# Attention over a graph: degree rows shared between two engines, and strip 0 checked early

## The chip, the cores and the metric

One Trainium2 chip, one core of it. The time is that of the device in microseconds (us) from launch to end; the profile's span runs from the first to the last instruction of one profiled execution. A core has TensorE (PE; its weight loads are listed as PEld), VectorE (DVE), ScalarE (ACT), GpSimd (POOL) and SyncE (SP, here used only to issue transfers). Each engine works through its own queue in order; semaphores tie the queues together.

## The reference

A graph of 2708 nodes with 128 features each: `x` (2708 x 128) and a dense 0/1 matrix `adj` (2708 x 2708, float32). Layer 0, which the change touches:

```
deg = clip(adj.sum(axis=1), 1);  dis = deg ** -0.5
diffusion = (dis[:, None] * adj * dis[None, :]) @ x - x
sim  = x @ x.T / (|x_i| |x_j|)
attn = softmax(beta * sim * adj, axis=1)
x = layernorm(x + diffusion + sigmoid(alpha) * (attn @ x - x))
```

Layer 1 is a second attention with `den = exp(leaky_relu(s_row + s_col))`, `att = den / (A @ den)`, `H = A @ (att @ (x W))`, and a last layernorm. It takes the larger part of the time and isn't changed.

## The kernel before

Nodes are cut into 22 blocks of 128 rows (the last has 20), and the columns of the transposed adjacency matrix into strips of 512 columns: strips 0 to 4, and a side strip 5 of 148 columns.

**Attention.** One loop runs over the strips in the order 2, 3, 4, 1, 0; I call its passes places 0 to 4. Place 4, the last, works on strip 0. In each place 22 steps `k` run over the blocks in the order 8 to 21, 4 to 7, 0 to 3 (`taken`). A step computes a 128 x 512 tile of similarities `sim` on PE (or turns one that an earlier place has kept), multiplies it on DVE with `gentle` (the limited beta) and with the block's piece of the adjacency matrix (`p_t`, line 651), takes the exponential in place on ACT (`grown`, 681), adds it on POOL to `total`, which becomes the softmax denominator, and multiplies it on PE with x into `att_acc` (`weighed`, 692). `p_t` has six buffers, `sim` four PSUM banks. Place 3 is wide: it carries the side strip along, and its `total` lies in `x1`, which has no other use yet.

The pieces of the current strip lie in `kept_a`, six tiles by groups of four blocks (2, 3, 4, 5, 1, 0 in the order of use); SP reloads each as soon as its last block is used. In place 4 there is no next strip to load.

**Degree rows.** `degree` (503) loads half a row block of `adj` (128 x 1354) into one of three rooms in turn and sums it on ACT into `deg2`. There are 44 of these; `rows_at` says at which steps of which place each is asked for. `roots` turns ready degrees into `dis` (DVE, then a power on POOL), at step 11 of place 2, step 20 of place 3 and step 12 of place 4. In place 4, at steps 11, 15, 19 and 21, x is scaled by `dis` on DVE (742), for blocks that att_acc no longer needs unscaled.

**What place 4 prepares.** `round_part(g)` copies a group of strip 0 into the matmul's rounded format on DVE; `check_part(g)` sums the low bits of the same pieces on ACT, so that a matrix that isn't exact in the short format is noticed; only then can `load_part(1, g)` let POOL's DMA queue load strip 1 into the group's place. `rounded_at` and `checked_at` hold the steps. Groups 2 and 3 of strip 1 are asked for at steps 17 and 20. Groups 1 and 0 are checked, and the other four loads are asked for, only after the place, behind the side strip's diffusion (1014 to 1021).

**Diffusion.** From line 1009 on PE multiplies each strip with x in two halves (`x_hi`, `x_lo`, made on DVE at 795 from the scaled x): side strip, 0, 1, 2, then 3 and 4. Strip s + 2 is loaded into the room of strip s as its parts are used up. `attended` finishes a strip of the attention: it sums `total` over the partitions on PE, turns `att_acc`, and adds the result to `att`. For strip 0 that is called after the side strip's diffusion and ahead of strip 0's in the text of the program.

**Order.** The order of each engine's queue is fixed when the program is built, by a planner that goes by the order of the text, its own costs and the times at which it thinks inputs are there. `in_order` pins a function's instructions behind the newest `p_t` product, exponential or addition of the place on their engine; they may be put later than that, not earlier. So the step numbers are the earliest places, not the real ones.

```
        def in_order(f):
            latest.update(behind)
            strict.append("some")
            f()
            strict.pop()
```

Of the kernel before, what the change touches and what calls it, by code (L numbers as in the profile page):

```python
# [12 lines left out]
I16 = mybir.dt.int16  # L13
AF = mybir.ActivationFunctionType
ALU = mybir.AluOpType
# [3 lines left out]
P = 128  # L19
N = 2708  # L20
D = 128
NB = (N + P - 1) // P
NP = NB * P
LAST = N - (NB - 1) * P
SW = 512
# [22 lines left out]
def grouped(  # L48
# [15 lines left out]
    nc = tc.nc  # L64
# [129 lines left out]
    def pinned(engine, op, *args, **kwargs):  # L194
        with ExitStack() as e:
            if engine in latest:
                e.enter_context(tc.issue_after(latest[engine].ins))
            latest[engine] = op(*args, **kwargs)  # L198
            return latest[engine]
# [9 lines left out]
    def dve(op, *args, **kwargs):  # L209
        if strict:  # L210
            return pinned("DVE", getattr(nc.vector, op), *args, **kwargs)
        return getattr(nc.vector, op)(*args, **kwargs)  # L212

    def act(op, *args, **kwargs):
        if strict:
            return pinned("ACT", getattr(nc.scalar, op), *args, **kwargs)
        return getattr(nc.scalar, op)(*args, **kwargs)  # L217

    def gps(op, *args, **kwargs):
        if strict:  # L220
            return pinned("POOL", getattr(nc.gpsimd, op), *args, **kwargs)
        return getattr(nc.gpsimd, op)(*args, **kwargs)  # L222
# [12 lines left out]
    def to_sbuf(acc, v, nb):  # L235

        t = lp.tile([P, SW], F32, tag="to_rows", name="tr_sb", bufs=2)
        if v < nb * P:
            nc.gpsimd.memset(t[:, v : nb * P], 0.0)
        act("copy", t[:, :v], acc[:, :v])  # L240
        return t
# [8 lines left out]
    def turned(t, nb):  # L250

        rows = tp_bank("tr_ps")
        for b in range(nb):
            mm(nc.tensor.transpose, rows[:, b, :], t[:, ts(b, P)], ident)
        return rows
# [78 lines left out]
    with ExitStack() as es:  # L334
# [161 lines left out]
# [4 lines that stand above are left out]
            f()  # L500
            strict.pop()

        def degree(ib, h):

            if (2 * ib + h) % 3 < 2:
                z = row_rooms[(2 * ib + h) % 3]
            else:
                z = x1[:, 6:, :].rearrange("p b i -> p (b i)")[:, : N // 2]
            nc.sync.dma_start(z, adj[ts(ib, P), h * (N // 2) : (h + 1) * (N // 2)])
            pinned(  # L510
                "ACT", nc.scalar.activation, z, z, AF.Copy,
                accum_out=deg2[:, ib, h : h + 1],
            )

        def roots(b0, b1):

            t = deg[:, b0:b1]
            dve("tensor_tensor", t, deg2[:, b0:b1, 0], deg2[:, b0:b1, 1], ALU.add)
            dve("tensor_scalar", live[:, b0:b1], t, 0.0, None, ALU.is_gt)
            dve("tensor_scalar", t, t, 1.0, None, ALU.max)  # L520
            gps("tensor_tensor", dis[:, b0:b1], t, minus_half[:, b0:b1], ALU.pow)

        def attended(s, acc, total):

            v, nb = width(s), blocks(s)
            sums = tp_bank("sums")
            for b in range(nb):
                nc.tensor.matmul(
                    sums[:, b, 0:1], total[:, ts(b, P)], ones[:, 0:1], start=True, stop=True
                )  # L530
            rsum = small.tile([P, SW // P], F32, tag="rsum", name="rsum")
            nc.vector.reciprocal(rsum[:, :nb], sums[:, :nb, 0])
            nc.vector.tensor_scalar(rsum[:, :nb], rsum[:, :nb], sig, None, ALU.mult)
            rows = turned(to_sbuf(acc, v, nb), nb)
            for b in range(nb):
                ib = s * 4 + b
                r = att[:, ib, :]
                nc.vector.scalar_tensor_tensor(
                    r, rows[:, b, :], rsum[:, b : b + 1], r, ALU.mult, ALU.add
                )  # L540


        room_of = {2: "room5", 3: "room1", 4: "room3", 1: "room0", 0: "room4", 5: "room2"}
        rounded_at = {2: 5, 3: 8, 4: 12, 1: 15, 0: 18, 5: 19}
        checked_at = {2: 13, 3: 18, 4: 21, 5: 21}
        strips = {0: {}, NS - 1: kept_c}

        def part_of(s, g):
# [7 lines left out]
        def round_part(g):  # L556
            dve("tensor_copy", part_of(0, g), kept_a[g])

        def check_part(g, room=None):
            low_bits_of(  # L560
                kept_a[g].rearrange("p b i -> p (b i)"),
                room or row_rooms[g % 2].bitcast(I16),
            )

        def load_part(s, g):
            src = adj_t[4 * g * P : min(4 * g + 4, NB) * P, ts(s, SW)]
            pinned(
                "strips", gps, "dma_start", part_of(s, g),
                src.rearrange("(b p) i -> p b i", p=P),
            )  # L570
# [6 lines left out]
        ended = []  # L577
        scaled = set()
        for n, s in enumerate(order):
# [2 lines left out]
            acc = ps_acc.tile([P, SW], F32, tag="acc", name="att_acc")  # L582
            if wide:
                total = x1[:, :6, :].rearrange("p b i -> p (b i)")
                nc.gpsimd.memset(total[:, w_all:], 1.0)
                tp_tags.remove("tp2")
                acc_side = ps_tp.tile([P, SW], F32, tag="tp2", name="att_acc_side")
            else:
                total = lp.tile([P, SW], F32, tag="total", name="total", bufs=2)
            gps("memset", total[:, :w_all], 0.0)  # L590

            prep = {
                (0, 1): lambda: normalize(12, 16),
# [6 lines left out]
                (1, 17): lambda: constants(2),  # L600
                (2, 11): lambda: roots(0, 8),
                (3, 20): lambda: roots(8, 18),
                (4, 12): lambda: roots(18, NB),
            }

            rows_at = {
                0: (18, 20), 1: range(0, NB, 2), 2: range(0, NB, 2),
                3: [k for k in range(21) if k % 3 < 2], 4: range(0, 12, 2),
            }
            turns = {  # L610
                3: lambda: turn_rows(12, 16, by_dve),
# [20 lines left out]
            for k, jb in enumerate(taken):  # L632
# [87 lines left out]
                if wide and k == 7:  # L720
                    in_order(lambda: attention_starts(NS - 1))
                if k in rows_at[n]:
                    in_order(lambda: degree(*todo.pop(0)))
                if n == len(order) - 1:
                    for g in [g for g, at in rounded_at.items() if at == k]:
                        in_order(lambda: round_part(g))
                    if k in (17, 20):
                        in_order(lambda: load_part(1, groups[k > 17]))
                    for g in [g for g, at in checked_at.items() if at == k]:
                        in_order(lambda: check_part(g))  # L730
                    if k in (11, 15, 19, 21):

                        done = sorted(taken[: k + 1 if k == NB - 1 else k - 1])
                        done = [b for b in done if b not in scaled]
                        scaled.update(done)
                        while done:
                            b0 = b1 = done[0]
                            while b1 in done:
                                done.remove(b1)
                                b1 += 1  # L740
                            xs = x_sb[:, b0:b1, :]
                            nc.vector.tensor_tensor(
                                xs, xs,
                                dis[:, b0:b1].unsqueeze(2).to_broadcast([P, b1 - b0, D]),
                                ALU.mult,
                            )
# [262 lines left out]
    for s in (NS - 1, 0, 1, 2):  # L1009
        acc = ps_acc.tile([P, SW], F32, tag="acc", name="dif_acc")  # L1010
        diffuse(s, acc)
        if s < 3:
            load_strip(s + 2)
        if s == NS - 1:
            attended(*ended.pop())
            for g in (1, 0):
                check_part(
                    g, work2.tile([P, 2048], I16, tag="low", name="low_junk", bufs=1)
                )
            for g in groups[2:]:  # L1020
                load_part(1, g)
        if s == 1:
            flat = kept_c.rearrange("p b i -> p (b i)")
            v = SHORT
            for b0, b1 in ((0, NB // 2), (NB // 2, NB)):
                low_bits_of(
                    flat[:, b0 * v : b1 * v],
                    work2.tile([P, 2048], I16, tag="low", name="low_junk", bufs=1),
                )
        normed(s, summed_up(s, acc))  # L1030
        x1_t = x1_in_sbuf(s, x1_turned(s))
        pbs = []
        for k in (1, 0):
            pb = scores(s, x1_t, k, score_bank())
            tally(s, pb, k)
            pbs.append(pb)
        shared_row(s, pbs[0])
        picked(s, pbs[0], sr_p)
        picked(s, pbs[1], sc_p)
        limited(s * 4, s * 4 + blocks(s))  # L1040
        e2(s * 4, s * 4 + blocks(s))
        if s == 1:
            fill("e")
# [1146 lines left out]
```

## Time and profile before

| what | us |
|---|---|
| median of 3 runs | 654.78 (653.06 to 657.62) |
| the profiled execution | 655.02 |
| its span | 653.6 |
| PE busy in the span | 611.0 (93%) |
| DVE busy | 492.1 (75%) |
| ACT busy | 471.1 (72%) |
| POOL busy | 291.2 (45%) |
| first p_t product of place 4 (DVE) | 175.0 |
| last p_t product of place 4 (DVE) | 207.7 |
| last att_acc product begins (PE) | 214.2 |
| first product of strip 0's diffusion (PE) | 221.1 |
| last degree row on ACT ends | 202.4 |

Lines of a timeline give the start, the duration, engine, source line, operation and its tiles; in brackets stands how long the engine was idle before and what released it. Many lines bear L198, L207 or L222, since these are the helpers that record every operation: tiles tell them apart. A busy share is an average over stages with different limits, and matmul ends are modelled, so PE can be shown busy where it partly waits.

### The profile page before, as it was taken

The page shows a single profiled execution, that of the slowest core. Times are in us where ns is not written, and L with a number is a line of the kernel's source. Part 1 is how long each engine was busy: PE and PEld are TensorE (multiplying, and loading weights), DVE is VectorE, ACT ScalarE, POOL GpSimd, SP SyncE. Part 2 cuts the span into 40 slices and gives each one's busy share as a digit, 9 for nine tenths or more (in the row PEclk, how much of TensorE's full clock was granted, in tenths as well). Part 3 has the DMA queues.
Part 4 walks back from the last instruction along what each step waited for, and adds up shares of the span by engine and source line. Part 5 has one row for each costly group of instructions (what it writes and reads, how often), then busy time and mean ns, then how long its engine had stood idle before and what let it go on. Part 6 is the DMA issues. An engine that isn't in the chain of part 4 may idle for free.

```text
span 653.6 us, 8554 instructions
## 1 busy us (share of the span) xinstructions
PE 611.0 (93%) x2859; PEld 354.7 (54%) x2859; DVE 492.1 (75%) x978; ACT 471.1 (72%) x649; POOL 291.2 (45%) x270
## 2 busy tenths in 40 slices
PE   8999999999999899988768899999999999989993
PEld 5445444475655676756645344444444444658872
DVE  4765875764699756757585999999999999498574
ACT  3857786777889521411376999999999999778662
POOL 5977778777798742000113323333232230022573
PEclk9999999999999899999879999999999999999997
DMA  8968989998972999988869997666689553359971
GB/s 273 385 209 319 323 291 366 357 342 299 335 260 76 274 389 390 386 274 301 330 247 251 252 231 234 183 180 177 195 216 266 173 165 128 98 206 384 390 296 53
DMA packets 66407, 171.64 MB, mean 263 GB/s; under 512 B 10059, under 2 KB 19285, under 8 KB 63333
## 3 DMA queue, kind: packets, MB, share of 16 engines
q1 hardware_dynamic: 42500, 107.01, 46.5%
q0 software_dynamic: 22464, 62.25, 33.9%
q10 hardware_dynamic: 1392, 1.77, 0.9%
q8 instruction: 24, 0.39, 0.2%
q14 instruction: 27, 0.21, 0.1%
HBM read 171.89 MB, written 5.72 MB: 272 GB/s over the span
## 4 chain that ended last, share of the span: by engine, by line
PE 75%; DVE 8%; POOL 6%; ACT 5%; issue 3%; DMA 2%; DVEq 0%; POOLq 0%; SPq 0%; ACTq 0%
PE num L198 15%; PE m_acc L198 15%; PE att_acc L207 9%; PE h_acc L1685 7%; PE sim L207 7%; PE dif_acc L207 6%; POOL total L222 4%; PE tot L198 2%; DMA nat<-in_adj_t 2%; PE sim L198 2%; DVE q L198 1%; PE dif_acc L198 1%; PE idle_ps L198 1%; ACT xn L198 1%; PE att_acc L198 1%
## 5 line engine op out<-in xcount | busy, mean ns | idle before, releaser
L198 PE MATMUL m_acc<-q,xws 128*128 128x512 f32 x240 | 121.6, 592 | 0.0
L222 POOL TENSOR_TENSOR total<-total,p_t 128x512 f32<-128x512 f32 (+1 forms) x67 | 91.7, 1369 | 21.0 <-ACT p_t L217 18.3
L198 PE MATMUL num<-ring,wt 128*128 128x512 f32 x216 | 98.1, 546 | 3.0 <-DVE q L198 2.2
L207 PE MATMUL att_acc<-p_t,x_sb 128*128 128x512 f32 x184 | 91.1, 602 | 1.1 <-ACT p_t L217 1.1
L212 DVE SCALAR_TENSOR_TENSOR p_t<-sim,gentle,pieces 128x512 f32<-128x512 f32 x89 | 65.0, 745 | 34.9 <-PE sim L207 25.7
L198 DVE SCALAR_TENSOR_TENSOR q<-sr_b,nc_s,q 128x1536 f32<-128x1536 f32 (+1 forms) x48 | 77.8, 1623 | 16.5 <-ACT q L198 16.5
L217 ACT ACTIVATE p_t<-p_t,shift 128x512 f32<-128x512 f32 (+1 forms) x89 | 64.7, 745 | 33.3 <-DVE p_t L212 31.0
L198 DVE COPY q<-num 128x512 f32<-128x512 f32 (+1 forms) x142 | 83.4, 611 | 3.7 <-PE num L198 3.7
L198 PEld LDWEIGHTS m_acc<-q,xws 128*128 128x128 f32 x240 | 45.3, 190 | 55.0 <-issue 55.0
L198 ACT ACTIVATE q<-q,head,rest 128x1536 f32<-128x1536 f32 (+1 forms) x48 | 70.2, 1508 | 1.5 <-DVE ring L198 1.2
L198 ACT ACT_TABLE_LOAD x52 | 66.7, 1283 | 3.9 <-issue 3.1
L198 PEld LDWEIGHTS num<-ring,wt 128*128 128x128 f32 x216 | 39.0, 190 | 48.4 <-issue 34.2
L198 ACT ACTIVATE q<-q,c_s 128x1536 f32<-128x1536 f32 (+1 forms) x48 | 62.9, 1355 | 0.3
L198 POOL DMA_INDIRECT ring<-in_adj_t,k_no x18 | 21.9, 1217 | 85.8 <-PE num L198 84.9
L207 PEld LDWEIGHTS att_acc<-p_t,x_sb 128*128 128x128 f32 x184 | 31.6, 190 | 35.4 <-ACT p_t L217 19.1
L207 PE MATMUL sim<-xn_t 128*128 128x512 f32 x98 | 47.6, 592 | 0.0
L222 POOL TENSOR_TENSOR x<-x,p_t 128x660 f32<-128x660 f32 (+1 forms) x22 | 35.1, 1595 | 11.3 <-ACT p_t L217 10.6
L198 ACT ACTIVATE row<-row 128x1354 f32<-128x1354 f32 x30 | 39.5, 1319 | 0.6 <-DMA row<-in_adj 0.6
L207 PE MATMUL dif_acc<-strip,x_hi 128*128 128x512 f32 x88 | 37.7, 429 | 0.0
L207 PE MATMUL dif_acc<-strip,x_lo 128*128 128x512 f32 x88 | 36.4, 414 | 0.0
L1685 PE MATMUL h_acc<-rounded,m_hi 128*128 128x512 f32 x88 | 32.5, 407 | 3.7 <-DVE rounded L212 3.7
L198 POOL DMA_INDIRECT xws<-xw_d,j_no x24 | 27.5, 1147 | 16.3 <-DVE c_s L198 9.3
(362 smaller groups left out, 1185.7 us busy)
## 6 DMA issues: line engine op xcount, KB each, us to landing
pieces<-in_adj_t SPq DMA_DIRECT2D x24, 1024.0 KB, 6.4
strip<-in_adj_t POOLq DMA_DIRECT2D x20, 1024.0 KB, 18.3
row<-in_adj SPq DMA_DIRECT2D x30, 677.0 KB, 6.0
nat<-in_adj_t SPq DMA_DIRECT2D x18, 768.0 KB, 6.1
x<-in_adj SPq DMA_DIRECT2D x14, 677.0 KB, 5.8
ring<-in_adj_t SPq DMA_DIRECT2D x9, 1024.0 KB, 5.1
x_sb<-in_adj_t SPq DMA_DIRECT2D x5, 768.0 KB, 6.3
pieces<-in_adj_t SPq DMA_DIRECT2D x7, 512.0 KB, 5.8
```

Of the source, the lines that this page charges most:

```text
L198: latest[engine] = op(*args, **kwargs)
L207: op(*args, **kwargs)
L212: return getattr(nc.vector, op)(*args, **kwargs)
L217: return getattr(nc.scalar, op)(*args, **kwargs)
L222: return getattr(nc.gpsimd, op)(*args, **kwargs)
L1685: nc.tensor.matmul(acc[:, : rows.shape[-1]], m[:, kb, :], rows, start=(kb, part) == (0, 0), stop=(kb, part) == (NB - 1, 1),)
```

## The change

Five edits, all in the attention's loop and right behind it:

- `degree` takes a flag; where it is set, the half row is summed by a DVE scalar operation with an accumulated sum instead of by ACT. `rows_by_dve` names the steps. The rows' steps change too: more in places 1 and 2, three instead of six in place 4.
- The last `roots` goes from step 12 to step 7 of place 4.
- `rounded_at` and `checked_at` get earlier steps, and all six groups are checked within the place, in the row rooms. A new table `asked_at` asks for each group of strip 1 some steps behind its check.
- The two memsets of the wide `total` are pinned at the start of place 3.
- `attended` of strip 0 is called after strip 0's diffusion; only its copy of `att_acc` to SBUF stays behind the side strip's.

```
-        def degree(ib, h):
+        def degree(ib, h, by_dve):
...
-            pinned(
-                "ACT", nc.scalar.activation, z, z, AF.Copy,
-                accum_out=deg2[:, ib, h : h + 1],
-            )
+            into = deg2[:, ib, h : h + 1]
+            if by_dve:
+                dve("tensor_scalar", z, z, 1.0, 0.0, ALU.mult, ALU.add, accum_out=into)
+            else:
+                act("activation", z, z, AF.Copy, accum_out=into)
...
-        def attended(s, acc, total):
+        def attended(s, acc, total, t=None):
...
-            rows = turned(to_sbuf(acc, v, nb), nb)
+            rows = turned(t or to_sbuf(acc, v, nb), nb)
...
-        rounded_at = {2: 5, 3: 8, 4: 12, 1: 15, 0: 18, 5: 19}
-        checked_at = {2: 13, 3: 18, 4: 21, 5: 21}
+        rounded_at = {2: 3, 3: 5, 4: 8, 1: 11, 0: 14, 5: 18}
+        checked_at = {2: 4, 3: 6, 4: 9, 1: 12, 0: 15, 5: 19}
+        asked_at = {2: 9, 3: 10, 4: 13, 1: 16, 0: 19, 5: 21}
...
-                nc.gpsimd.memset(total[:, w_all:], 1.0)
+                in_order(lambda: gps("memset", total[:, w_all:], 1.0))
...
-            gps("memset", total[:, :w_all], 0.0)
+            if wide:
+                in_order(lambda: gps("memset", total[:, :w_all], 0.0))
+            else:
+                gps("memset", total[:, :w_all], 0.0)
...
-                (4, 12): lambda: roots(18, NB),
+                (4, 7): lambda: roots(18, NB),
...
-                0: (18, 20), 1: range(0, NB, 2), 2: range(0, NB, 2),
-                3: [k for k in range(21) if k % 3 < 2], 4: range(0, 12, 2),
+                0: (18, 20), 1: (*range(0, NB, 2), 21), 2: (*range(0, NB, 2), 5, 13),
+                3: [k for k in range(21) if k % 3 < 2], 4: (0, 2, 4),
+            }
+            rows_by_dve = {
+                0: (), 1: (4, 8, 12, 16, 20), 2: (2, 5, 8, 11, 13, 14, 20),
+                3: (1, 4, 7, 10, 13, 16, 19), 4: (0, 2, 4),
...
-                    in_order(lambda: degree(*todo.pop(0)))
+                    in_order(lambda: degree(*todo.pop(0), k in rows_by_dve[n]))
...
-                    if k in (17, 20):
-                        in_order(lambda: load_part(1, groups[k > 17]))
                     for g in [g for g, at in checked_at.items() if at == k]:
                         in_order(lambda: check_part(g))
+                    for g in [g for g, at in asked_at.items() if at == k]:
+                        in_order(lambda: load_part(1, g))
...
         if s == NS - 1:
-            attended(*ended.pop())
-            for g in (1, 0):
-                check_part(
-                    g, work2.tile([P, 2048], I16, tag="low", name="low_junk", bufs=1)
-                )
-            for g in groups[2:]:
-                load_part(1, g)
+            in_sbuf = to_sbuf(ended[0][1], SW, SW // P)
+        if s == 0:
+            attended(*ended.pop(), in_sbuf)
```

More of the change, by code (lines that the diff above doesn't have):

```diff
@@ L557, in round_part, with check_part @@
             dve("tensor_copy", part_of(0, g), kept_a[g])
-        def check_part(g, room=None):
+        def check_part(g):
             low_bits_of(
                 kept_a[g].rearrange("p b i -> p (b i)"),
-                room or row_rooms[g % 2].bitcast(I16),
+                row_rooms[g % 2].bitcast(I16),
             )
```

## The prediction

> **What bounds the kernel now.** I read the page first, then the windows by stage, the chain of waits, and the timelines of DVE and PE around the end of the last place. The windows by place of the attention (places 1 to 3, place 4, the gap to the diffusion, the diffusion) give, in us, PE, PEld, DVE, ACT and POOL busy with their counts, the granted clock, the DMA share and GB/s:
>
> ```profile
> 50.00:92.00 42.00, 41.99 (x120) 19.16 (x119) 30.41 (x60) 30.82 (x48) 30.50 (x26) 1.00 0.87 316
> 92.00:129.00 37.00, 36.69 (x120) 18.23 (x119) 23.46 (x41) 26.85 (x42) 29.92 (x24) 1.00 1.00 360
> 129.00:174.00 45.00, 44.70 (x203) 28.46 (x201) 27.41 (x56) 33.91 (x47) 33.93 (x22) 1.00 0.90 322
> 174.00:209.00 35.00, 34.38 (x153) 20.65 (x152) 31.28 (x47) 31.82 (x50) 30.71 (x21) 1.00 0.63 209
> 209.00:221.00 12.00, 8.13 (x48) 6.05 (x47) 9.64 (x7) 8.13 (x11) 11.70 (x13) 1.00 0.45 118
> 221.00:290.00 69.00, 67.61 (x302) 48.94 (x303) 44.55 (x215) 19.54 (x30) 15.77 (x22) 0.98 1.25 364
> ```
>
> Places 1 to 3 are TensorE's: 0.6 us idle in 124. In place 4 DVE (31.3 of 35) and ACT (31.8) are as full. Then 12 us with PE partly idle, then 69 us of diffusion in which PE is busy again. The gap is the only cheap time here. The timeline of PE in it (start, duration, what, idle before and its releaser):
>
> ```profile
> 211.41 0.77 PE L207 MATMUL dif_acc<-side,x_sb 128*128 128x148 f32 x4 [1.31 <-DVE x_sb L742]
> 212.02 2.74 PE L207 MATMUL att_acc<-p_t,x_sb 128*128 128x512 f32 x6
> 214.59 2.68 PE L207 MATMUL dif_acc<-side,x_sb 128*128 128x148 f32 x20
> 220.05 1.05 PE L528 MATMUL sums<-ones,total 128*128 128x1 f32 x8 [2.56 <-POOL total L222]
> 221.14 0.48 PE L207 MATMUL dif_acc<-strip,x_hi 128*128 128x512 f32 x1
> ```
>
> PE stood 1.31 us for the scaled x and 2.56 us for POOL's row sum, and strip 0 begins at 221.1. The timeline of DVE shows a second thing that ends there:
>
> ```profile
> 205.78 1.23 DVE L198 TENSOR_TENSOR deg<-deg 128x4 f32<-128x4 f32 x1
> ...
> 209.60 3.43 DVE L742 TENSOR_TENSOR x_sb<-x_sb,dis 128x512 f32<-128x512 f32 x2 [1.13 <-POOL dis L198]
> 214.79 0.69 DVE L742 TENSOR_TENSOR x_sb<-x_sb,dis 128x512 f32<-128x512 f32 x1 [1.76 <-PE att_acc L207]
> 215.40 2.91 DVE L212 CAST x_hi<-x_sb 128x384 fp32r<-128x384 f32 x2
> 218.24 2.92 DVE L212 TENSOR_TENSOR x_lo<-x_sb,x_hi 128x384 fp32r<-128x384 f32 x2
> ```
>
> The first half that strip 0 needs, x_lo of blocks 8 to 10, takes 2.19 us by its group's row and is ready at about 220.4, 0.7 us before PE takes it. So both chains end together: freeing PE of the row sum alone brings 0.7 us, not 2.56. Afterwards matmuls run at half pace (0.43 us apart instead of 0.23) from 222.4 to 225.9, some eight of them: 1.7 us lost to the clock after that idle time.
>
> **The parts, and what each costs.**
>
> Rows. 44 half rows are summed, today all on ACT. By the new sets place 1 has 12 (11 before), place 2 has 13 (11), place 3 has 14, place 4 has 3 (6). DVE takes 5, 6, 7 and 3 of them: 21 of 44 (step 11 of place 2 is listed, but no row stands there). An ACT row is 1.32 + 0.1 us until the next instruction, so ACT is relieved of 21 x 1.41 = 29.6 us. In places 1 to 3 nothing waits for ACT longer than PE does: gain 0. The DVE form (scalar operation with a sum) isn't in the trace from SBUF. The same form from PSUM is:
>
> ```profile
> L212 DVE TENSOR_SCALAR_CACHE_REDUCE junk<-sb_ps,ntheta 128x512 f32<-128x512 f32 x6 | 4.3, 749 | 2.8 <-PE sb_ps L207 2.8
> L212 DVE TENSOR_SCALAR_CACHE_REDUCE junk<-sb_ps,ntheta 128x148 f32<-128x148 f32 x2 | 0.7, 368 | 0.1
> ```
>
> That is 1.047 ns an element, so 1354 elements are 1.63 us, and since such instructions start 0.675 us apart where they last 0.75, one row holds DVE 1.55 us. Below: by the rounding (2048 elements in 1.21 us) 0.8 us. Above: the scaling of x beside POOL (1280 in 2.35) 2.5 us. I take 1.55, the same instruction. The Trainium skill, "SBUF — State Buffer", "Who interferes with whom", says that a scalar operation writing out its sum does not enter the mode that locks POOL out, while casts do. The casts here show the lock (POOL's additions are 1.27 us alone and 2.1 to 2.4 beside one); no row shows the sum form from SBUF. If the rule failed, POOL would lose up to 21 x 1.55 us; by the rule nothing.
>
> In places 1 to 3 the cover is DVE's idle time. 30.41 + 5 x 1.55 = 38.2 of 42; 23.46 + 9.3 = 32.8 of 37; 27.41 + 10.85 = 38.3 of 45. It fits, at 85 to 91%. Behind a row that waits for its transfer or merely runs stand the next p_t product, behind it ACT's exponential and PE's att_acc. Floor 0. Ceiling, if PE had no step in hand: DVE has 42.7 us idle over 66 steps, 0.65 a step; a row costs 1.55 - 0.65 = 0.9, times 18 = 16.2 us. Nearest row: all ACT rows together waited 0.6 us for transfers, and PE already lets DVE wait for sim. I take 1.0 us. SP issues three row transfers more in places 1 and 2 and three fewer in place 4; piece loads queue behind them, and DMA has 316 to 360 GB/s there against 388 in the diffusion: 0.
>
> Place 4. DVE is asked for 3 x 1.55 = 4.65 us more before strip 0 can start. Against it, waits that the change removes: 1.13 us (dis comes early, since the last roots move from step 12 to 7 and have fewer rows ahead), 0.72 us (deg of blocks 8 to 17 waiting for an ACT row at 178.95), and 1.76 us (after the products, now that the scaling and halves follow without the ACT checks). 4.65 - 3.6 = 1.0 us later. Casts and checks are the same number, only earlier: 0 each; ACT loses 9 rows' worth of work there and its six checks (1.9 + 0.1 us, one 1.1) all fit, 11 us beside 22 x 0.64 of exponentials in 35.
>
> The row sum. The sums and turns of strip 0's attention (1.05 + 0.4 us of PE) move behind strip 0's diffusion, into a train where PE is the bound: +1.45; the 0.7 us shown above goes: together +0.75. The copy to SBUF stays where it was: 0.
>
> Strip 1. Its six loads are asked for from step 9 on instead of from step 17 with four after the place: first issue near 196 instead of 212.4, into DMA engines that are empty from 199 to 210. But no PE wait in 220 to 290 names a strip, so the gain is 0 as long as PE sets the diffusion; the ceiling is 14 us (5.5 MB at 388 GB/s). POOL issues four more inside the place, 0.74 to 0.98 each, so its last addition ends near 223 instead of 220; PE no longer waits for that before 231: 0, or up to 3.9 if p_t's buffers run out. Here a page speaks against the change: the same page, "SBUF: two separate sides", warns that descriptors of POOL's DMAs starve while DVE runs two-port casts, and the casts stand exactly there. By the trace the two issues near the gap took 0.98 and 0.78 against 0.74 later; by the page each of six could lose a cast, 1.2 us, 7 us of POOL in sum.
>
> Memsets of the wide total go from 3.3 us to the start of place 3: 0.64 + 0.18 us of POOL, which is 75% busy there: 0, else 0.8.
>
> The clock. PE is still without work for some us before strip 0, so I leave its 1.7 us in.
>
> Sum: 1.0 + 1.0 + 0.75 = +2.8 us on the profiled execution's 655.0 (span 653.6): 657.8. The median of the runs, 654.8, is the same within 0.2 us.
>
> **Rivals.**
>
> *DVE becomes the bound in places 1 to 3 (slower).* For it: DVE at 85 to 91% in one queue, each row more than two steps' slack. Against: PE has up to four sim banks. It decides once att_acc finds its exponential late after a row; at half of the ceiling 8.1, plus 1.8 from place 4 and the sums: 665.
>
> *The gap closes (faster).* If halves are ordered into DVE's free moments before the last scaling, strip 0 can begin at 217.5, right behind the side strip: -3.6, no clock loss -1.7, no 1.31 stop: -6.6, with the +0.7 of moved sums: 649. For it: x's scaling no longer waits for dis, and no check is late. Against: DVE's total.
>
> *The rows lag as today.* After 175.0 ACT ran nine rows though place 4 asks for six. With the same lag of three, DVE gets two of them, 3.1 us more: 661.
>
> *The diffusion was fed too late (faster).* If DMA, busy at 388 GB/s from 216 to 281, is the true bound, the early strip is worth most of 14: 644. Against: PE waits for no strip.
>
> **How the numbers follow.** Forecast 0.42, range 652 to 662; DVE bound 0.24; gap closes 0.20; lag 0.09; feeding 0.05. 1% is 6.5 us, about what a measurement can tell from no change. Faster by over 1%: feeding and 0.08 of the gap case, 0.13. Slower: DVE bound and 0.03 of the lag, 0.27. Same 0.60. The range leaves out the feeding case and the far end of the DVE case: 648 to 666.
>
> **What would show it.** Right: a DVE row group at 1.5 to 1.65 us; PE idle in places 1 to 3 of 1 to 2 us; first strip 0 product at 221 to 224; first strip issue before 200; sums after strip 0; half clock once more near it. Wrong: PE idle for p_t of 5 us or more before 174 (DVE bound), strip 0 before 219 (gap closes), a diffusion shorter than 67 us (feeding).

## The result and the profile after

The changed kernel takes 672.45 us (median of 6 runs, 671.91 to 675.34) against 655.45 (6 runs, 653.06 to 661.04) for the kernel before beside it: 1.0259 times as long, 95% interval 1.0219 to 1.0298. It is slower by 17 us; forecast were 3. Some executions fall into a slower state with a lower granted clock: medians below count them, ratios leave them out, and e6's trace is of one.

The profiled execution has a span of 669.8 us (before: 653.6). Marks in the two traces:

| mark, us | before | after |
|---|---|---|
| first side product of place 3 (DVE) | 129.5 | 128.0 |
| last side product of place 3 (DVE) | 173.2 | 176.9 |
| last p_t product of place 4 (DVE) | 207.7 | 223.3 |
| last att_acc product begins (PE) | 214.2 | 229.1 |
| first product of strip 0's diffusion | 221.1 | 230.3 |
| last strip product of this diffusion | 290.1 | 306.1 |
| span | 653.6 | 669.8 |

The after trace starts its attention 1.75 us earlier, for a reason that has nothing to do with the change (last section). With that taken off, places 1 and 2 cost 0.25 us more, place 3 (first to last side product) costs 5.2 more and place 4 (from there to the last p_t product) 11.9. From the last p_t product to the last att_acc product it is 0.7 shorter, from there to the last strip product 1.1 longer, and all that follows is the same within 0.3. So the loss arises in places 3 and 4.

The windows by stage, after (PE, PEld, DVE, ACT, POOL busy with counts, granted clock, DMA share, GB/s):

```profile
50.00:92.00 42.00, 40.96 (x119) 18.75 (x118) 34.00 (x68) 23.92 (x37) 29.60 (x25) 1.00 0.87 308
92.00:129.00 37.00, 36.99 (x123) 18.71 (x122) 28.92 (x48) 23.38 (x36) 31.03 (x26) 1.00 0.96 355
129.00:174.00 45.00, 42.38 (x186) 26.25 (x186) 33.06 (x61) 24.64 (x33) 30.66 (x22) 1.00 0.88 303
174.00:209.00 35.00, 29.96 (x128) 17.04 (x126) 32.77 (x48) 14.56 (x22) 25.67 (x18) 0.95 0.66 234
209.00:221.00 12.00, 10.43 (x42) 5.98 (x43) 11.43 (x18) 10.48 (x13) 7.55 (x7) 1.00 0.47 125
221.00:290.00 69.00, 64.04 (x272) 45.62 (x271) 46.15 (x173) 25.16 (x37) 26.31 (x32) 0.95 1.17 335
```

In the fourth line ACT has lost half its work (31.8 to 14.6) and PE is idle for 5.0 us instead of 0.6. DVE is busy for 32.8 of 35 us, and for 11.4 of the next 12: it is the bound now. The waits from 176 to 235 us name the chain (who waited, for whom: us in total, times, longest):

```profile
ACT p_t L217 <- DVE p_t L212: 21.4, 11, 5.9
PEld att_acc L207 <- ACT p_t L217: 9.5, 15, 2.0
```

Before, from 176 to 222 us, the first of these lines was:

```profile
ACT p_t L217 <- DVE p_t L212: 3.1, 5, 1.7
```

The timeline of DVE in the last part of place 4 and the gap, after, shows what DVE did instead of p_t (its first three lines, a cast, a scaling and a row in a train, stand in the longest wait, of 5.9 us):

```profile
202.85 2.07 DVE L198 CAST strip<-pieces 128x2048 fp32r<-128x2048 f32 x1
204.85 2.55 DVE L751 TENSOR_TENSOR x_sb<-x_sb,dis 128x1280 f32<-128x1280 f32 x1
207.32 1.55 DVE L198 TENSOR_SCALAR_CACHE_REDUCE x<-x 128x1354 f32<-128x1354 f32 x1
...
209.46 1.55 DVE L198 TENSOR_SCALAR_CACHE_REDUCE row<-row 128x1354 f32<-128x1354 f32 x1
...
212.26 1.55 DVE L198 TENSOR_SCALAR_CACHE_REDUCE row<-row 128x1354 f32<-128x1354 f32 x1
...
213.74 1.22 DVE L198 CAST strip<-pieces 128x2048 fp32r<-128x2048 f32 x1
214.88 0.15 DVE L198 TENSOR_TENSOR deg<-deg 128x4 f32<-128x4 f32 x1
...
225.45 1.93 DVE L751 TENSOR_TENSOR x_sb<-x_sb,dis 128x512 f32<-128x512 f32 x1 [1.43 <-PE att_acc L207]
227.30 3.02 DVE L212 CAST x_hi<-x_sb 128x384 fp32r<-128x384 f32 x2
230.24 3.98 DVE L212 TENSOR_TENSOR x_lo<-x_sb,x_hi 128x384 fp32r<-128x384 f32 x2
234.14 0.68 DVE L751 TENSOR_TENSOR x_sb<-x_sb,dis 128x512 f32<-128x512 f32 x1
```

DVE ran six rows in place 4 (at 183.95, 189.74, 199.14 and the three shown), though the program asks for three there. The last one ends at 213.8; the last row of before ended on ACT at 202.4. So `deg` is complete at 214.9, where it was at 205.8, for all that `roots` is asked for five steps earlier. Then the last lines: four halves of x stand ahead of the last scaling of x (234.14). The timeline of PE in the gap shows who needs that scaling:

```profile
232.46 0.50 PE L207 MATMUL dif_acc<-strip,x_lo 128*128 128x512 f32 x1 [1.62 <-DVE x_lo L212]
234.87 2.34 PE L207 MATMUL dif_acc<-side,x_sb 128*128 128x148 f32 x8 [1.91 <-DVE x_sb L751]
...
249.57 0.94 PE L529 MATMUL sums<-ones,total 128*128 128x1 f32 x8
```

PE's queue still holds eight products of the side strip. They wait for DVE, and strip 0 waits behind them: it has begun at 230.3, but runs only from 237. The last line is the moved row sum, now behind strip 0's diffusion. The timeline of ACT, after, at the end of place 4:

```profile
209.64 0.72 ACT L217 ACTIVATE p_t<-p_t,shift 128x512 f32<-128x512 f32 x1 [5.93 <-DVE p_t L212]
211.05 1.91 ACT L198 ACTIVATE row<-pieces 128x2048 int16<-128x2048 int16 x1 [0.70 <-DVE row L198]
...
213.85 1.91 ACT L198 ACTIVATE row<-pieces 128x2048 int16<-128x2048 int16 x1 [0.18 <-DVE row L198]
...
215.76 1.89 ACT L198 ACTIVATE row<-pieces 128x2048 int16<-128x2048 int16 x1
...
217.66 1.89 ACT L198 ACTIVATE row<-pieces 128x2048 int16<-128x2048 int16 x1
...
219.55 1.32 ACT L217 ACTIVATE p_t<-p_t,shift 128x512 f32<-128x512 f32 x2
```

`row<-pieces` is a check. The first was asked for at step 4 of 22 and runs at 211.05, later than before (202.40). Its releaser says why: the check writes what it throws away into a room of the degree rows, and the rows still stand there. And on POOL, the first load of strip 1:

```profile
213.37 1.91 POOL L198 DMA_DIRECT2D strip<-in_adj_t  x1 [1.59 <-ACT row L198]
```

It came at 212.43 before. So the early tables have moved neither the checks nor the loads forward.

### The profile page after: what moved, and what is told of

It is laid out like the page before. It is cut to its first block, busy times and chain, and to the rows that moved or that the text cites. A ratio compares the mean times of both kernels' runs of the same rounds, so it can differ in the third digit from the quotient of the medians.

```text
span 669.8 us, 8555 instructions
## 1 busy us (share of the span) xinstructions
PE 617.8 (92%) x2859; PEld 355.4 (53%) x2859; DVE 522.5 (78%) x1020; ACT 447.7 (67%) x609; POOL 290.0 (43%) x270
## 4 chain that ended last, share of the span: by engine, by line
PE 70%; DVE 14%; ACT 6%; issue 5%; POOL 3%; DMA 2%; DVEq 0%; ACTq 0%; SPq 0%; POOLq 0%
PE num L198 15%; PE m_acc L198 15%; PE att_acc L207 8%; PE h_acc L1690 7%; PE dif_acc L207 7%; PE sim L207 6%; DVE p_t L212 3%; PE tot L198 2%; DMA nat<-in_adj_t 2%; ACT p_t L217 1%; DVE row L198 1%; DVE q L198 1%; PE dif_acc L198 1%; PE sb_ps L207 1%; PE sim L198 1%
## 5 line engine op out<-in xcount | busy, mean ns | idle before, releaser
L222 POOL TENSOR_TENSOR total<-total,p_t 128x512 f32<-128x512 f32 (+1 forms) x67 | 89.4, 1335 | 25.5 <-ACT p_t L217 22.8
L207 PE MATMUL att_acc<-p_t,x_sb 128*128 128x512 f32 x184 | 93.7, 618 | 5.9 <-ACT p_t L217 5.4
L207 PEld LDWEIGHTS att_acc<-p_t,x_sb 128*128 128x128 f32 x184 | 31.8, 192 | 43.1 <-ACT p_t L217 26.3
L198 PE MATMUL num<-x_sb,wt 128*128 128x512 f32 (+1 forms) x72 | 34.2, 568 | 0.7 <-ACT gb L198 0.7
```

## The experiments

In all there are two suspects, DVE's rows and the early preparation (checks, casts, loads, order of the halves, row sum). The pinned memsets and the new row steps were not run alone; they are in e1, whose place 3 takes 44.2 us against 43.7 before, and in e8, which is as fast as before. A ratio is against runs of the kernel before on the same chip; those lay at 654.5 to 656.7 us. In the diffs, a kernel called "change" is the changed one.

The last column is read from each run's trace: the time from the first side product of place 3 (DVE) to the last strip product of the diffusion (PE). It leaves out the start of the program and layer 1, which differ between executions (last section). It is 160.6 us before and 178.1 in the change. Kernels profiled twice differ in it by 0.1 (e13, e17), 0.9 (change, e16) and 1.7 us (e2, e18).

| run | kernel | median, us | ratio, 95% interval | mark to mark, us |
|---|---|---|---|---|
| e1 | change, all rows on ACT | 661.54 | 1.0116 (1.0023 to 1.0209) | 168.0 |
| e2 | before, with the rows alone | 665.63 | 1.0150 (1.0060 to 1.0240) | 172.5 |
| e3 | change, DVE rows only in places 1, 2 | 664.03 | 1.0130 (1.0048 to 1.0212) | 170.1 |
| e4 | change, DVE sums half of each row | 664.12 | 1.0161 (1.0063 to 1.0259) | 169.5 |
| e5 | before, row sum moved | 656.64 | 0.9991 (0.9945 to 1.0037) | 161.2 |
| e6 | before, early tables | 665.34 | 1.0117 (1.0036 to 1.0198) | - |
| e7 | e1 with own rooms for checks | 659.88 | 1.0058 (1.0014 to 1.0101) | 165.6 |
| e8 | e7 with late halves | 655.73 | 0.9985 (0.9951 to 1.0020) | 161.0 |
| e9 | e1 with late halves | 660.42 | 1.0107 (1.0045 to 1.0169) | 163.9 |
| e10 | change, DVE rows only in places 3, 4 | 665.01 | 1.0168 (1.0111 to 1.0225) | 174.4 |
| e11 | e5 with late halves | 652.84 | 0.9971 (0.9940 to 1.0003) | 159.5 |
| e12 | e8 with later checks | 662.72 | 1.0103 (1.0063 to 1.0143) | 167.9 |
| e13 | change, own rooms, late halves | 672.93 | 1.0235 (1.0158 to 1.0311) | 172.0 |
| e14 | before, late halves | 656.77 | 0.9996 (0.9959 to 1.0032) | 160.6 |
| e15 | e11 with early casts | 656.32 | 1.0002 (0.9965 to 1.0039) | 158.3 |
| e16 | change, beside the next two | 673.34 | 1.0310 (1.0256 to 1.0363) | 177.2 |
| e17 | e13 again | 667.65 | 1.0196 (1.0157 to 1.0234) | 172.1 |
| e18 | e2 again | 670.30 | 1.0251 (1.0199 to 1.0302) | 174.2 |

### Which suspect: e1 and e2

e1 takes DVE's rows out of the change; e2 puts the rows, their new steps and the earlier roots into the kernel before, and nothing else.

```
e1, to change:
-            rows_by_dve = {0: (), 1: (4, 8, 12, 16, 20), ...}
+            rows_by_dve = {n: () for n in range(5)}
e2, to before:
-        def degree(ib, h):
+        def degree(ib, h, by_dve):
...
+            rows_by_dve = {0: (), 1: (4, 8, 12, 16, 20), ...}
```

> The changed kernel with every degree row summed by ACT again; the rows' steps, the early rounding, checks and strip 1 loads and the late row sum of strip 0 stay. Theory A (DVE has too much to do in places 3 and 4 once it sums rows): nearly all of the 16 us goes, 650 to 657 us, place 4 lasts 31 to 35 us from its first to its last p_t product on DVE (32.6 before, 44.7 after). Theory B (the early rounding, checks and loads in place 4 are what costs): 664 to 670 us, place 4 still 40 us or more.

> The kernel before with only the rows edit: the new row steps, 21 rows on DVE, the last roots at step 7; rounding, checks, strip 1 loads, memsets and the row sum as before. Theory A: 667 to 673 us, place 4 at least 41 us. Theory B: 655 to 660 us, place 4 33 to 37 us.

Measured: 661.5 and 665.6. Both are guilty. The rows cost 9.5 us (e2 against before) or 10.9 (change against e1); the rest costs 5.4 (e1 against before) or 6.8 (change against e2). No single-cause theory holds. In e1 the preparation can be seen without the rows; its ACT ran four checks in a row from 204.89 to 212.4, ahead of the exponentials of the last steps, and the timeline of PE there reads:

```profile
210.65 2.31 PE L207 MATMUL dif_acc<-side,x_sb 128*128 128x148 f32 x8 [2.98 <-DVE x_sb L748]
213.22 4.99 PE L207 MATMUL att_acc<-p_t,x_sb 128*128 128x512 f32 x10 [0.26 <-ACT p_t L217]
...
224.63 2.34 PE L207 MATMUL dif_acc<-side,x_sb 128*128 128x148 f32 x8 [5.41 <-DVE x_sb L748]
```

Ten products of att_acc come in one train at 213, since their exponentials were behind the checks; then 5.4 us of waiting for a scaling of x that stands behind halves.

### What of the rows: e3, e4, e10

```
e3, to change:
-                3: (1, 4, 7, 10, 13, 16, 19), 4: (0, 2, 4),
+                3: (), 4: (),
e4, to change:
-                dve("tensor_scalar", z, z, 1.0, 0.0, ALU.mult, ALU.add, accum_out=into)
+                dve("tensor_scalar", z[:, : N // 4], z[:, : N // 4], 1.0, 0.0, ...)
e10, to change:
-                0: (), 1: (4, 8, 12, 16, 20), 2: (2, 5, 8, 11, 13, 14, 20),
+                0: (), 1: (), 2: (),
```

> The changed kernel with rows on DVE in places 1 and 2 alone (11 of them; places 3 and 4 on ACT). Theory A: rows cost nothing where DVE has time, so within 2 us of the kernel with all rows on ACT; if rows that lag cross into place 3, up to 4 us more. Theory B: like the kernel with all rows on ACT, 664 to 670. A third theory (each row on DVE costs the same wherever it stands, 16 / 21 = 0.76 us): 8 us over the kernel with all rows on ACT.

> The changed kernel with DVE's 21 rows summed over 677 of their 1354 columns only (the other half of these sums is left out, so degrees are too small). Each DVE row should last 0.85 us instead of 1.55. Theory A: the thirteen rows that DVE runs in places 3 and 4 give back 13 x 0.7 = 9 us at most, 662 to 667 us. Theory B or a cost per row that is a wait rather than DVE's time: 670 to 673 us.

> The changed kernel with DVE's rows in places 3 and 4 alone (10 of 21 rows), those of places 1 and 2 on ACT. Rows in places 1 and 2 alone cost 2.5 us against none, and those of places 3 and 4 on top of them 8.4. Theory A1, the later rows are dear because the earlier ones push them back into the last place: without the earlier ones place 4 has no more than four rows on DVE and ends 5 us or more earlier, 662 to 665. Theory A2, DVE has no room in places 3 and 4 itself, and each of the 10 rows costs about 0.84 us there: place 4 is as long as in the changed kernel, 668 to 671.

e4 leaves out half of the sums that are on DVE. It gave back 8.3 us of the change's 17, for 21 rows of 0.85 us instead of 1.55 (15 us of DVE time less): what a row costs is mostly DVE's time, not its transfer, which is as large as ever. (In the change two rows of place 2 did wait for their transfers, 1.25 and 0.95 us, but places 1 and 2 lost only 0.25.)

e3 measured 664.0 and e10 665.0, against 661.5 with no row on DVE and 672.4 with all. By these medians eleven early rows alone cost 2.5 us, ten late ones alone 3.5, and both 10.9. That would make a row dearer the more rows stand before it, but with four runs each the intervals of e1, e3 and e10 overlap, and the marks don't bear it out: 2.1 us for the early rows, 6.4 for the late ones, and 10.1 for both (9.2 by e16), which is near the sum. e10 was to tell whether the later rows are dear only because earlier ones push them into the last place. Its time (665) is where that theory had it, at its upper edge; its mechanism is not right as put. Six rows still ran on DVE in place 4, and place 4, from the last side product to the last p_t product, took 45.5 us, about as long as in the change (46.3), which is what the other theory said. The first of the six began at 181.39, the last at 209.27. So DVE's rows lag by three in place 4 whichever engine had the earlier ones. Place 3 shows the push: it took 43.7 us before (first to last side product), 48.0 in e3, which asks for no DVE row there but ran three late ones of place 2 (130.54, 133.24, 144.47), 48.9 in the change, and 45.8 in e10, where place 2 has none. Most of what place 3 loses comes from rows that belong to place 2.

### What of the preparation: e5, e6, e7, e8, e9

```
e5, to before (row sum only):
-            attended(*ended.pop())
+            in_sbuf = to_sbuf(ended[0][1], SW, SW // P)
...
+        if s == 0:
+            attended(*ended.pop(), in_sbuf)
e6, to before (tables only):
+        rounded_at = {2: 3, 3: 5, ...}; checked_at = {2: 4, 3: 6, ...}; asked_at = {2: 9, ...}
own rooms (e7, e8, to e1):
+        junk_of = {2: "room1", 3: "room3", 4: "room0", 1: "room4"}
...
+            if g in junk_of:
+                room = strip_b.tile([P, 4, SW], F32, tag=junk_of[g], name="turned")
late halves (e8, e9, to e7 and e1):
-                            nc.vector.tensor_tensor(
+                            latest["DVE"] = nc.vector.tensor_tensor(
...
+    strict.append("halves")
     for b0, b1 in ((8, 11), (11, 16), (16, NB), (4, 8), (0, 4)):
         halves(x_part(0, b0, b1), x_part(1, b0, b1), x_sb[:, b0:b1, :])
+    strict.pop()
```

> The kernel before with one part of the change alone: the last attended side's copy out of the accumulator stays behind strip 15's work, and its row sum, reciprocal and the rest go behind strip 0. Rows, rounding, checks and strip 1's loads are as before. The early part and the moved row sum together were worth about +5.4 us against before (all rows on ACT: 661.5 against 656.1). Theory B1, the cost is in the rounding, checks and loads: this kernel is at the level of before, 655 to 657. Theory B2, the cost is in the moved row sum: 660 to 662.

> The kernel before with the other half of that part: strip 0 is rounded, checked and strip 1 asked for by the tables of the change, while the row sum stays where it was and all rows are on ACT. Theory B1: 660 to 662, with a bunch of checks ahead of the last exponentials on ACT and PE waiting 3 us or more for x. Theory B2: 655 to 657.

> The changed kernel with all rows on ACT (661.5 us measured), and the checks of four of the six groups write what they throw away into rooms of the diffusion's strips that are free, instead of the rooms of the degree rows. Theory C1, the checks come late because they wait for the rows' rooms, and then stand in a bunch of 7 to 9 us ahead of the last exponentials: the first check runs before 195 us, the last side of p_t is done 3 to 5 us earlier, 657 to 659. Theory C2, it is the halves of x ordered ahead of the last scaling that hold PE (5.4 us at one product): the checks run early all the same, and the time stays at 660 to 662.

> As the kernel with own rooms for the checks, and the halves of x are held behind the last scaling of x on DVE, so that PE's last side products do not wait for a scaling that stands behind halves. Theory C1 alone: the same as with own rooms, 657 to 659. Theory C2 alone: 656 to 657, 5 us under the 661.5 of the kernel with all rows on ACT. Both: 653 to 655, at or under the kernel before.

> The changed kernel with all rows on ACT (661.5 us) and the halves of x behind the last scaling, the checks still in the rows' rooms: it completes the square of own rooms (659.9), own rooms and late halves (655.7). Theory D1, the two causes add: 656.5 to 658, about 4 us under 661.5 from the halves, and the five checks ahead of the last exponentials remain on ACT with PE's last side of p_t at 217. Theory D2, late halves help only where the checks are early: 660 to 662.

The moved row sum costs nothing that e5 can show, and the early tables alone cost as much as e1 (e6, 1.2% both). Two edits were tried on e1. Own rooms let the first check run at 181.82 us, where e1 had it at 201.68, and the last att_acc product begins at 213.9 instead of 217.6; yet the time falls by 1.7 us only, since PE then waits 5.2 us at the side strip's last products. Late halves alone take 1.1 us: the checks still hold the last exponentials. With both, the loss is gone (655.7, equal to before). The timeline of PE in e8:

```profile
214.47 3.10 PE L207 MATMUL dif_acc<-side,x_sb 128*128 128x148 f32 x22
217.74 0.47 PE L207 MATMUL dif_acc<-strip,x_hi 128*128 128x512 f32 x1 [0.16 <-DVE x_hi L198]
219.87 0.50 PE L207 MATMUL dif_acc<-strip,x_lo 128*128 128x512 f32 x1 [1.67 <-DVE x_lo L198]
```

The side strip goes through in one train of 22, and strip 0 follows. So there are two causes: the checks delay attention, and the order of the halves delays the diffusion. Either edit alone leaves the other's wait standing. The intervals of e1, e7 and e9 overlap, so the times can't tell whether the two add; by the marks own rooms alone give back 2.4 us, late halves alone 4.1, and both 7.0, which is near the sum.

### A better version: e11, e12, e14, e15

If the order of the halves matters, the kernel before may gain from it. e11 is e5 with late halves; e14 has the late halves without the moved row sum; e15 is e11 with the change's `rounded_at`; e12 is e8 with these checks:

```
-        checked_at = {2: 4, 3: 6, 4: 9, 1: 12, 0: 15, 5: 19}
-        asked_at = {2: 9, 3: 10, 4: 13, 1: 16, 0: 19, 5: 21}
+        checked_at = {2: 9, 3: 14, 4: 19, 1: 21, 0: 21, 5: 21}
+        asked_at = {2: 11, 3: 16, 4: 21, 1: 21, 0: 21, 5: 21}
```

> The kernel before with the row sum moved (no change by itself, 0.999) and the halves of x ordered high, low, high, low behind the last scaling; rounding, checks, loads and rows as before. There PE waited 3.0 us for the first low half, since two high halves of 384 and 640 columns stood ahead of it. Theory D3, the gap between attention and diffusion counts: the wait is 1 to 1.7 us and the time 1 to 1.5 us under before, 654.5 to 656. Theory D4, strip 1's landing sets the start of the next strip in any case: no change, 656 to 657.

> The kernel before with the halves of x ordered high, low behind the last scaling, and the row sum where it was, ahead of strip 0 on PE. With the row sum moved the same edit measured 652.8 against 655.5. Theory G1, the moved row sum is a gain once the halves are ready earlier, since PE otherwise waits for POOL's last addition until 220: no change here, 655 to 656.5. Theory G2, the order of the halves does it alone: 652.5 to 654.

> The kernel with moved row sum and late halves (652.8), and strip 0 rounded at the early steps of the change; checks and loads as in the kernel before. Theory H1, the casts are the same number of instructions in another place and cost nothing: 652 to 654. Theory H2, DVE's casts ahead of its share of p_t hold PE in the middle of the last place: 1 to 3 us more, 654 to 656.

> The version with own rooms and late halves, rounding as early as in the change, but only three of the six checks ahead of the last step (steps 9, 14 and 19 instead of 4 to 19); the others come behind the last exponentials, as in the kernel before. Theory D5, every check in the last place costs its ACT time there, since ACT is 30.8 of 34 us busy: attention ends 1 to 2 us earlier than with the early checks, strip 0 starts with it, and the time is 1 to 2 us under both that version and before, 653 to 655. Theory D6, the loads of strip 1 come too late by it: 656 to 658.

e11 is the best median of all, 652.8 against 655.5, but its interval reaches 1.0003: a gain of 0.3% that this measurement doesn't quite tell from none. The traces point the same way. PE, in e11 and then in e14:

```profile
216.91 0.50 PE L207 MATMUL dif_acc<-strip,x_lo 128*128 128x512 f32 x1 [0.93 <-DVE x_lo L198]
```

```profile
218.62 1.05 PE L528 MATMUL sums<-ones,total 128*128 128x1 f32 x8 [2.55 <-POOL total L222]
```

With late halves the first low half is ready near 216.9. In e14 PE stands at the row sum until 218.6 and starts strip 0 at 219.8; in e11 nothing stands between, and the last strip product begins at 287.5 instead of 288.7. So, by one trace each, the moved row sum is worth about 1.1 us where the halves are early enough, and nothing where they are not (e5). e15 was inconclusive: 1.0002 with an interval that holds both theories.

e12 was a miss by its own edit. A room of strip 0 is free for a check only until that room's own group is rounded into it; with checks at steps 9 to 21 the rounding came first. In the timeline of ACT its first own-room check runs at

```profile
223.99 1.91 ACT L198 ACTIVATE turned<-pieces 128x2048 int16<-128x2048 int16 x1 [2.15 <-PE dif_acc L207]
```

that is, when PE had used the strip up, and PE then waited for strip 1 four times (0.84, 0.89, 0.54 and 2.47 us, each named `DMA strip<-in_adj_t`). It says nothing on how many checks place 4 can hold; it does show that loads which begin at 226.3 instead of e8's 196.3 come too late.

### Do the two costs add: e13, e16, e17, e18

e13 and e17 are the change with both edits of e8, its rows still on DVE.

> The changed kernel, its rows on DVE and all, with own rooms for four checks and the halves of x behind the last scaling. With all rows on ACT these two edits took 661.5 to 655.7. Theory F1, rows and early checks are two costs that add: 5 to 7 us under the changed kernel's 672.4, 665 to 667.5, and still 9 to 11 us over before. Theory F2, the rows on DVE are dear only because they hold the rooms of the checks: 656 to 660. Theory F3, with the rows on DVE the last place is so full that the checks cost nothing more: 670 to 673.

> The changed kernel itself, on the same chip as the next two, as their yardstick: 671 to 674.

> The changed kernel with own rooms for the checks and late halves, once more: its trace ends the diffusion 4.5 us earlier than the change's, its time of 672.9 did not show it. Theory F1, the two costs add: 4 to 6 us under the yardstick. Theory F3: within 2 us of it.

> The kernel before with the rows on DVE alone, once more (665.6 measured): Theory F1: 5 to 7 us under the yardstick, and no better than the version with own rooms and late halves by more than 2 us. Theory F3: as far under the yardstick, and the mended checks still cost 5 us or more against it.

e13's 672.9 would say that with DVE's rows the mended preparation brings nothing, but its trace ended the diffusion at 301.6 instead of 306.1. On one chip e17 is at 667.7 against 673.3, and the two intervals are apart: the edits give back 5.7 us here too, as they gave 5.8 without the rows (by the marks 5.1 and 7.0). That is what costs that add would give, and e13's four runs were too few. e18 (670.3) missed the 5 to 7 us under the yardstick; it is 3.0 under it, so a part of the preparation's cost may be hidden behind the rows. So what remains of the change's 17 to 19 us after the preparation is mended is the rows: 13.9 us by e17 against e8 (1.0196 over 0.9985), 15.8 by e18, 9.5 by e2. The marks give 11.1, 13.6 and 11.9 for the same pairs. I can't place it better than 10 to 16.

## Why the prediction was wrong

The prediction went wrong where it priced DVE's rows at 2.0 us (1.0 in places 1 to 3, 1.0 in place 4), which cost 10 to 16, and where it put the early casts and checks at 0: with the order of the halves that came with them they cost 5.4 (e1).

**Rows in places 1 to 3, "I take 1.0 us".** Failed; with the next step it holds most of the loss. The duration was right: estimated 1.55, measured

```profile
L198 DVE TENSOR_SCALAR_CACHE_REDUCE row<-row x14: 1546/1554/1564, 56.0 to 212.3; 128x1354 f32<-128x1354 f32 x14
```

(shortest, median, longest, in ns). The cover was wrong. Idle time of DVE was counted as room, and it is not room where it lies between a product and the sim that the next one needs. PE was idle for 3.7 us in places 1 to 3 (forecast 1 to 2), nearly all in places 1 and 3, and place 3 as a whole lost 5.2. The waits from 129 to 178 us, after and then before, name who was late:

```profile
ACT p_t L217 <- DVE p_t L212: 20.3, 17, 2.7
```

```profile
ACT p_t L217 <- DVE p_t L212: 9.2, 9, 1.8
```

DVE was at 73% in the window of place 3 all the same. A share of busy time said "it fits"; the order said no. Places 1 to 3 lost 5.4 us in all, 0.3 a row, between the floor of 0 and the ceiling of 0.9. The rival "DVE becomes the bound" had the mechanism, but named a place too early: places 1 and 2 pay a quarter of a microsecond, 3 and 4 the rest, and its sign, 5 us of PE idle before 174, did not come. That its ceiling of 16.2 us is near the measured loss is luck.

**Place 4, "4.65 - 3.6 = 1.0 us later".** Failed in both terms. DVE ran six rows, not three: 9.3 us. The trace of before had shown the lag (nine ACT rows after 175.0, where six were asked for), and the rival "the rows lag as today" was built on it, but it gave DVE two of them and priced them at their own time. And of the waits that the change was to remove only 1.7 us went: DVE still stood 0.51 us for `dis` (217.66) and 1.43 for att_acc (225.45), where it had stood 1.13 and 1.76; the 0.72 for `deg` is gone. `dis` waits for the last row, which was later by 11.4 us.

**Casts and checks, "the same number, only earlier: 0 each", "all fit".** Failed. The sum of ACT's times did fit, but the checks could not run early because they write into the row rooms, and then stood in a bunch ahead of exponentials. The step that was missing is to ask where each moved instruction writes and who holds that place. With the casts nothing was found (e15).

**"First issue near 196 instead of 212.4".** Failed for the same reason: 213.4. Where rooms are free, e8 issues its first load at 196.3. That nothing is gained by it was right: e8's diffusion takes 68.8 us from the first train of strip 0 (219.9) to its last strip product, before 69.0.

**The row sum, +0.75.** Not shown wrong. e5's total (0.9945 to 1.0037) can't tell +0.75 from none, but its trace does what was worked out: its first x_lo product waits 2.96 us for DVE, and it takes 161.2 us from mark to mark against 160.6. With late halves the trace shows 1.1 us gained instead (e11 against e14).

**The rival "the gap closes".** Its order came true (halves ahead of the last scaling) with the opposite sign: PE's queue has the side strip's last products ahead of strip 0, and they need that scaling. Worth 5.4 us of waiting in e1.

**POOL and DVE.** The Trainium skill, "SBUF — State Buffer", "Who interferes with whom", lets POOL run beside a scalar operation with an accumulated sum. This trace agrees: POOL's addition at 98.46 lies wholly beside the row of 98.31 and took 1.28 us, and the median of the additions of 512 columns is 1275 ns before and after. The same page's "SBUF: two separate sides" warned of slow descriptors beside casts. The issue at 213.37 (shown above) took 1.91 us with a cast beside it at 213.74, the other five 0.74 to 0.93; that is one of six, not the seven microseconds that it would be if each lost a cast, and no run shows that the cast was its reason.

**The clock.** Half clock came near the gap as forecast, and once more inside place 4: the eight-microsecond slices at 200 and 232 have 0.79 and 0.59 of full clock, some 5 us of it, where before has 1.7 at 216 to 231. What set it off is not shown: PE was busy for 6.25 and 6.54 of the 8 us ahead of these two slices, but also for 6.24 of the 8 us from 216, and the slice after that kept full clock.

## What to carry to other kernels

Work moved to an engine with idle time is free only if it can stand where that idle time is; ask for the instruction behind it in the queue and how many products lie ready for the engine after, not for the share. When instructions are moved forward, look at every tile that they read and write, scratch included: a room that another late chain holds keeps them where they were, and they then run in a bunch. And an in-order queue makes the order of small preparations count: here high and low halves that overtook one scaling cost, by the marks, 4.1 us, more than the 2.4 of the late checks.

## What the runs showed of the hardware that was not expected

The start of the program differs by 1.5 to 2 us between executions of the same instructions: four warm-up products took 2.06 us in the trace of before and 2.05 in that of e13, and 1.11 in that of the change, where TensorE's products reached their shorter time earlier. And layer 1, which no kernel here changes, took 210.5 us from the first to the last `m_acc` product before and after the change, 213.4 in e13, 214.3 in e12 and 218.3 in e17. So for edits of a few microseconds marks within the trace say more than one total, and several runs on one chip are needed to say it with the total.
